# Pairwise products of a row: two pieces ahead of the loop, and a loop that begins with the third

## The chip, the core and the metric

The kernel runs on one core of a Trainium2 chip. The metric is the device time of one execution in microseconds; the profile that is read here was taken of one of the executions whose times are given. TensorE has no part in this kernel. The engines that matter are VectorE (DVE in the profile), ScalarE (ACT), SyncE (SP, which issues all the DMAs) and the sixteen DMA engines of the core.

## What is computed

The input is a matrix of 4096 rows and 256 columns in float32. For each row the outer product of the row with itself is formed, and its upper triangle is written out, row of the triangle after row of the triangle: 256 products with the first element, 255 with the second, and so on, 32,896 numbers in all.

```python
dot = jnp.einsum('bi,bj->bij', inputs, inputs)
iu, ju = jnp.triu_indices(d)
return dot[:, iu, ju]
```

4 MB are read and 539 MB are written. A run of the triangle (row i) is the tail of the input row, from element i on, times the one number x[i].

## The kernel before

**Tiling.** The 4096 rows are spread over 128 partitions, 32 to each. Two of them (REPEAT) are worked on at a time in every partition, so there are 16 groups. The width of 32,896 is cut into three pieces (PIECES, L115): c = 0 has 10,944 columns, c = 1 and c = 2 have 10,976 each. Each piece of a group is computed into one of two buffers, `places[0]` and `places[1]` (L128), and stored by one DMA of 11 MB. The first piece holds few long runs, the third many short ones.

**Sharing.** Of every piece, ACT computes the first runs and DVE the rest. `split` (L69) takes runs from DVE until DVE's time by a formula (L65: 68 ns and 1.046 ns an element, for one instruction over both rows) is within a budget of nanoseconds, or until ACT's time by its own formula (L74: 184 ns and 0.837 ns an element, one instruction for each of the two rows) is more than what is left to DVE. The budget is 0.9 times twice the columns (L204). A budget of 0 means an even split. DVE issues `tensor_tensor` products (L158), ACT an `activation` Copy with a scale (L170). Both read their own copy of the rows, `xv` and `xa`, which they refresh ahead of each c = 0 (L193 and L195).

**Order.** `rounds` (L178) writes out six pieces, two groups, for all engines. Piece p goes to buffer p mod 2. Before it is computed, DVE takes the buffer's semaphore `free` (L198), which the landing store of the piece two before has raised, and tells ACT by `go` (L199, L200). When DVE and ACT have marked their parts done (`v_done` L207, `a_done` L211), SP takes both marks and issues the store (L214). So at most two stores are under way, and a piece is computed while the store of the piece before it runs.

`rounds` is written out once ahead of the loop (L223) and is the body of a loop of seven passes over DVE, ACT and SP together (L224), whose head is put at the start of a code block on DVE and ACT (`head_slot`, L229). Ahead of the loop two things differ. The first two pieces wait for no buffer. And piece 0 is cut at columns 512, 1536 and 3584 (FIRST, L20), so that its first store can leave early; its four parts are shared evenly (L204, `start`), and each has its store. Piece 1 is shared by the budget of 0.9 like the rest. The input comes in three loads on SP (L138), the first of them only the rows of the first group; the others are waited for ahead of the second group (L188).

At the end SP takes both buffers' semaphores (L233), that is, waits for the last two stores, and lowers the loads' semaphores (L235).

Of the kernel before, what the change touches and what calls it, by code (L numbers as in the profile page):

```python
# [8 lines left out]
F32 = mybir.dt.float32  # L9
AF = mybir.ActivationFunctionType  # L10
ALU = mybir.AluOpType

P = 128
UNIT = 32
REPEAT = 2
PIECES = 3
PLACES = 2
ROUNDS = 2
BUDGET = 0.9
FIRST = [512, 1536, 3584]  # L20
ENGINES = OrderedEngineSet([mybir.EngineType.DVE, mybir.EngineType.Activation, mybir.EngineType.SP])


def even_borders(lo: int, hi: int, pieces: int) -> list[int]:
# [4 lines left out]
def runs(d: int, lo: int, hi: int) -> list:  # L29


    found, at = [], 0
    for i in range(d):
        a, b = max(at, lo), min(at + d - i, hi)
        if a < b:
            found.append((i, i + a - at, a, b - a))
        at += d - i
    return found


def vector_ops(block: list) -> list:

    ops, k = [], 0
    while k < len(block):
        i, j, at, n = block[k]
        m = 2 if k + 2 < len(block) and i == j else 1
        ops.append((block[k], m))  # L50
        k += m
    return ops


def interleave(block: list) -> list:


    half = len(block)
    while half and len(vector_ops(block[:half])) > len(vector_ops(block[half:])):
        half -= 1  # L60
    a, b = vector_ops(block[:half]), vector_ops(block[half:])
    return [op for k in range(max(len(a), len(b))) for ops in (a, b) for op in ops[k : k + 1]]


def vector_time(block: list) -> float:  # L65
    return sum(68 + 1.046 * REPEAT * n * m for (*_, n), m in vector_ops(block))


def split(block: list, budget: float) -> int:  # L69


    scalar, k = 0.0, 0
    while k < len(block):
        scalar += REPEAT * (184 + 0.837 * block[k][3])  # L74
        if vector_time(block[k:]) <= budget or scalar > vector_time(block[k + 1 :]):
            break
        k += 1
    return k


def window(ap: bass.AP, free: list) -> bass.AP:
    return bass.AP(ap.tensor, ap.offset, [list(ap.ap[0]), *free])


class Count:

    def __init__(self, ctx: ExitStack, nc, name: str):
        self.sem = ctx.enter_context(nc.semaphore(name))  # L90

    def take(self, engine, value: int):
        engine.wait_ge(self.sem, value).then_inc(self.sem, -value)  # L93


@with_exitstack
def kernel(
    ctx: ExitStack, tc: tile.TileContext, x: bass.AP, out: bass.AP
):

    nc = tc.nc
    n, d = x.shape  # L110
    width = out.shape[1]
    groups = n // (P * REPEAT)
    assert n % (P * REPEAT) == 0 and width == d * (d + 1) // 2 and width % UNIT == 0
    assert groups % ROUNDS == 0 and ROUNDS * PIECES % PLACES == 0
    borders = even_borders(0, width, PIECES)  # L115
    spans = list(zip(borders, borders[1:]))
    slot = max(b - a for a, b in spans)

    x_in = x.rearrange("(p g) d -> p (g d)", p=P)
    x_out = out.rearrange("(p h q r) c -> h q p r c", p=P, q=ROUNDS, r=REPEAT)  # L120

    each = REPEAT * d
    pool = ctx.enter_context(tc.tile_pool(name="all", bufs=1))
    xt = pool.tile([P, groups // ROUNDS, ROUNDS * each], F32, name="x")

    xv = pool.tile([P, each + 1], F32, name="xv")
    xa = pool.tile([P, each], F32, name="xa")
    places = [pool.tile([P, REPEAT, slot], F32, name=f"o{k}") for k in range(PLACES)]  # L128
    ctx.enter_context(tc.tile_critical())  # L129

    loads = [0, each, groups // 2 * each, groups * each]
    loaded = [ctx.enter_context(nc.semaphore(f"loaded{k}")) for k in range(len(loads) - 1)]
    free = [Count(ctx, nc, f"free{k}") for k in range(PLACES)]
    go, v_done, a_done = (Count(ctx, nc, name) for name in ("go", "v_done", "a_done"))
    v_own, a_own = (ctx.enter_context(nc.semaphore(name)) for name in ("v_own", "a_own"))

    for (a, b), sem in zip(zip(loads, loads[1:]), loaded):
        nc.sync.dma_start(xt.rearrange("p h d -> p (h d)")[:, a:b], x_in[:, a:b]).then_inc(sem, 16)  # L138

    class VectorWork:  # L140


        count = 0

        def add(self, ins, back: int = 1):
            if self.count > back:
                ins._wait_ge(v_own, self.count - back)
            ins.then_inc(v_own, 1)
            self.count += 1

        def end(self, back: int = 0):
            nc.vector.wait_ge(v_own, self.count)

    def vector_part(work: VectorWork, o, lo: int, block: list):
        for (i, j, at, length), m in interleave(block):
            at -= lo
            work.add(
                nc.vector.tensor_tensor(  # L158
                    o[:, :, at : at + m * length],
                    window(xv[:, j:], [[d, REPEAT], [1, m], [1, length]]),  # L160
                    window(xv[:, i:], [[d, REPEAT], [1, m], [0, length]]),
                    ALU.mult,
                )
            )

    def scalar_part(o, lo: int, block: list):
        ins = None
        for i, j, at, length in block:
            for r in range(REPEAT):
                ins = nc.scalar.activation(  # L170
                    o[:, r, at - lo : at - lo + length],
                    xa[:, r * d + j : r * d + j + length],
                    AF.Copy,
                    scale=xa[:, r * d + i : r * d + i + 1],
                )
        ins.then_inc(a_own, 1)

    def rounds(h, first: bool):  # L178

        work = VectorWork()  # L180
        for p in range(ROUNDS * PIECES):
            r, c = divmod(p, PIECES)
            k = p % PLACES
            lo, hi = spans[c]
            start = first and p == 0
            if c == 0:
                if first:
                    for sem in loaded[:1] if r == 0 else loaded[1:]:  # L188
                        nc.vector.wait_ge(sem, 16)
                        nc.scalar.wait_ge(sem, 16)  # L190
                x_now = xt[:, bass.ds(h, 1), r * each : (r + 1) * each]
                x_now = x_now.rearrange("p o d -> p (o d)")
                work.add(nc.vector.tensor_copy(xv[:, :each], x_now))  # L193
                work.end()
                nc.scalar.activation(xa, x_now, AF.Copy).then_inc(a_own, 1)  # L195
                nc.scalar.wait_ge(a_own, 1).then_inc(a_own, -1)
            if not (first and p < PLACES):
                free[k].take(nc.vector, 16 * stores[k])  # L198
                nc.vector.sem_inc(go.sem, 1)  # L199
                go.take(nc.scalar, 1)  # L200
            cuts = [lo, *(FIRST if start else []), hi]
            for a, b in zip(cuts, cuts[1:]):
                block = runs(d, a, b)
                share = split(block, 0.0 if start else BUDGET * REPEAT * (b - a))  # L204
                vector_part(work, places[k], lo, block[share:])
                work.end()
                nc.vector.sem_inc(v_done.sem, 1)  # L207
                if share:
                    scalar_part(places[k], lo, block[:share])
                    nc.scalar.wait_ge(a_own, 1).then_inc(a_own, -1)  # L210
                nc.scalar.sem_inc(a_done.sem, 1)  # L211
                v_done.take(nc.sync, 1)
                a_done.take(nc.sync, 1)
                nc.sync.dma_start(  # L214
                    x_out[bass.ds(h, 1), r, :, :, a:b].rearrange("o p r c -> p (o r) c"),
                    places[k][:, :, a - lo : b - lo],
                ).then_inc(free[k].sem, 16)
            stores[k] = len(cuts) - 1
        nc.vector.sem_inc(v_own, -work.count)

    stores = [0] * PLACES
    nc.vector.memset(xv[:, each:], 0.0)  # L222
    rounds(0, first=True)  # L223
    with nc.Fori(  # L224
        1,
        groups // ROUNDS,
        1,
        engines=ENGINES,
        head_slot={mybir.EngineType.DVE: 0, mybir.EngineType.Activation: 0},  # L229
    ) as h:  # L230
        rounds(h, first=False)
    for k in range(PLACES):
        free[k].take(nc.sync, 16)  # L233
    for sem in loaded:
        nc.sync.sem_inc(sem, -16)  # L235


# [25 lines left out]
```

## Time and profile before

| what | value |
|---|---|
| median of 4 executions | 1275.72 us (1275.56 to 1275.79) |
| the profiled execution | 1275.68 us, its span 1273.7 us |
| DVE, ACT busy | 952.5 us (1748 instructions), 535.2 us (1601) |
| stores of a whole piece, issue to landing, median | 31.9 us |
| DMA rate over the span | 426 GB/s |

The page begins with the busy time and its share of the span for every engine. Then the span is shown in forty slices; in the DMA row a digit is the mean busy share of the sixteen DMA engines in tenths, 9 for 90% or more. The part on queues gives the packets, their bytes and the time that they took; "instruction" packets bring program code of 8 KB each. A timeline row is a group of like instructions that follow each other: its start, its length, engine, line, what is written from what, how many, and in brackets the idle time of the engine before the first of them, with what ended it ("issue" is a wait for nothing that the profile shows). SPq, DVEq and ACTq are the sequencers of the engines, which wait and count semaphores. Besides, the trace holds a record for each DMA packet (start, length, bytes) and for each of the sixteen landing marks of a store.

### The profile page before, as it was taken

How to read it: one execution, taken by the hardware profiler on the slowest of the kernel's cores; microseconds unless marked ns; L12 is line 12 of the kernel's file. 1: busy time of each engine (PE TensorE's matmuls, PEld its weight loads, DVE VectorE, ACT ScalarE, POOL GpSimd, SP SyncE). 2: the span in 40 equal slices, each digit the busy share in tenths (PEclk: the TensorE clock that was granted, in tenths of full speed). 3: DMA queues.
4: the chain of work that ended last, by engine and by line, in shares of the span. 5: the costliest groups of instructions: out<-in, count | busy, mean ns of one | idle time of the engine just before them, and what ended most of it. 6: DMA issues, size and time to landing. Idle time of an engine off the chain costs nothing. (4 is left out here: it accounts for less than half of the span.)

```text
span 1273.7 us, 4059 instructions
## 1 busy us (share of the span) xinstructions
DVE 952.5 (75%) x1748; ACT 535.2 (42%) x1601; POOL 0.2 (0%) x4
## 2 busy tenths in 40 slices
DVE  8967787688867887678867787687877878678770
ACT  7524525245253442544326342263523625245250
POOL 0000000000000000000000000000000000000000
DMA  9999999999999999999999999999999999999997
GB/s 380 411 420 439 423 435 440 421 439 425 435 440 423 436 423 437 440 420 441 421 439 440 420 439 422 437 423 436 423 438 421 440 418 441 419 440 419 440 419 335
DMA packets 14314, 543.25 MB, mean 427 GB/s; under 512 B 864, under 2 KB 864, under 8 KB 1504
## 3 DMA queue, kind: packets, MB, share of 16 engines
q1 hardware_dynamic: 14304, 543.17, 99.2%
q14 instruction: 10, 0.08, 0.0%
HBM read 4.19 MB, written 538.97 MB: 426 GB/s over the span
## 5 line engine op out<-in xcount | busy, mean ns | idle before, releaser
L158 DVE TENSOR_TENSOR o<-xv 128x672 f32<-128x672 f32 (+27 forms) x1731 | 945.6, 631 | 268.9 <-DVEq L93 268.3
L170 ACT ACTIVATE o<-xa 128x253 f32<-128x253 f32 (+49 forms) x1584 | 523.8, 423 | 686.4 <-ACTq L93 685.6
L193 DVE COPY xv<-x 128x512 f32 (+1 forms) x16 | 6.8, 427 | 17.4 <-issue 8.2
L195 ACT ACTIVATE xa<-x 128x512 f32 (+1 forms) x16 | 10.1, 630 | 13.5 <-issue 6.1
L195 ACT ACT_TABLE_LOAD x1 | 1.3, 1283 | 0.9 <-SPq L129 0.9
L222 DVE MEMSET xv<- 128x1 f32 x1 | 0.1, 59 | 1.0 <-SPq L129 1.0
L250 POOL MEMSET const-bfloat16-1.0<- 128x1 bf16 x1 | 0.1, 101 | 0.0
L250 POOL MEMSET const-uint8-127<- 128x1 uint8 x1 | 0.1, 101 | 0.0
L250 POOL MEMSET const-float32-0.0<- 128x1 f32 x1 | 0.1, 98 | 0.2 <-issue 0.2
L250 POOL MEMSET const-float32-1.0<- 128x1 f32 x1 | 0.1, 98 | 0.0
## 6 DMA issues: line engine op xcount, KB each, us to landing
out_dram<-o SPq DMA_DIRECT2D x32, 10976.0 KB, 31.9
out_dram<-o SPq DMA_DIRECT2D x15, 10944.0 KB, 31.9
out_dram<-o SPq DMA_DIRECT2D x1, 7360.0 KB, 19.2
x<-in_r_inputs_dram SPq DMA_DIRECT2D x1, 2048.0 KB, 12.3
out_dram<-o SPq DMA_DIRECT2D x1, 2048.0 KB, 11.7
x<-in_r_inputs_dram SPq DMA_DIRECT2D x1, 1792.0 KB, 6.9
out_dram<-o SPq DMA_DIRECT2D x1, 1024.0 KB, 10.0
out_dram<-o SPq DMA_DIRECT2D x1, 512.0 KB, 9.7
```

Source lines behind the costliest of these rows:

```text
L158: nc.vector.tensor_tensor(o[:, :, at : at + m * length], window(xv[:, j:], [[d, REPEAT], [1, m], [1, length]]), window(xv[:, i:], [[d, REP ...
L170: ins = nc.scalar.activation(o[:, r, at - lo : at - lo + length], xa[:, r * d + j : r * d + j + length], AF.Copy, scale=xa[:, r * d + i : ...
L193: work.add(nc.vector.tensor_copy(xv[:, :each], x_now))
L195: nc.scalar.activation(xa, x_now, AF.Copy).then_inc(a_own, 1)
L222: nc.vector.memset(xv[:, each:], 0.0)
L250: nc = _bacc.Bacc("TRN2", target_bir_lowering=False, num_devices=1)
```

## The change

Ahead of the loop only pieces 0 and 1 are written out, and both are shared evenly between DVE and ACT; piece 0 keeps its four parts. The loop now has eight passes. A pass opens with pieces 2 to 5 of its two groups and goes on with pieces 0 and 1 of the next two groups; these last two stand in an If that the last pass jumps over. Each of the three engines has its own loop, so the program of each is written by a function of its own (`vector`, `scalar`, `sync`), and the waits on the second and third input loads come ahead of the loop. In the loop the budget is 0.95, 0.8 and 0.85 for the three kinds of piece instead of 0.9 for all. The stores of piece 0's four parts raise a semaphore `head`, and GpSimd, which had no part in the kernel, waits for it and raises `free[0]` in their place, so that the loop can always wait for one store.

In the built program, the first branch of ACT stands between its wait for the first load and the load of its activation table; formerly the table load came ahead of that wait. The loop has 243 instructions on DVE (242 before) and 249 on ACT (223 before); a piece takes, on DVE and ACT:

| piece | before: products on DVE, instructions on ACT | after, ahead of the loop | after, in the loop |
|---|---|---|---|
| c = 0 | 20, 18 (ahead of the loop 20, 34) | 20, 34 | 21, 14 |
| c = 1 | 26, 26 | 21, 44 | 23, 36 |
| c = 2 | 61, 54 | none | 59, 62 |

(These are counts of the sharing's own lists; the program has one product more in places.)

```diff
-ROUNDS = 2
-BUDGET = 0.9
+PASS = 6
+AHEAD = 2
+BUDGETS = [0.95, 0.8, 0.85]
...
+    def blocks(p: int, ahead: bool):
+        lo, hi = spans[p % PIECES]
+        cuts = [lo, *(FIRST if ahead and p == 0 else []), hi]
+        for a, b in zip(cuts, cuts[1:]):
+            block = runs(d, a, b)
+            k = split(block, 0.0 if ahead else BUDGETS[p % PIECES] * REPEAT * (b - a))
+            yield a - lo, b - lo, block[:k], block[k:], lo
+
+    def vector(h, pieces: range, ahead: bool):
+        for p in pieces:
+            if p % PIECES == 0:
+                v.add(nc.vector.tensor_copy(xv[:, :each], x_of(h, p // PIECES)), 0)
+                v.end()
+            if not ahead:
+                take(nc.vector, free[p % PLACES], 16)
+                nc.vector.sem_inc(go, 1)
+            for _, _, _, block, lo in blocks(p, ahead):
...
+                v.end().then_inc(v_done, 1)
+        v.restart()
+
+    def scalar(h, pieces: range, ahead: bool):
+        for p in pieces:
+            if p % PIECES == 0:
+                a.add(nc.scalar.activation(xa, x_of(h, p // PIECES), AF.Copy), 0)
+                a.end()
+            if not ahead:
+                take(nc.scalar, go, 1)
+            for _, _, block, _, lo in blocks(p, ahead):
...
+                a.end().then_inc(a_done, 1)
+        a.restart()
+
+    def sync(h, pieces: range, ahead: bool):
+        for p in pieces:
+            place = places[p % PLACES]
+            parts = list(blocks(p, ahead))
+            for lo, hi, *_, base in parts:
+                take(nc.sync, v_done, 1)
+                take(nc.sync, a_done, 1)
+                to = x_out[bass.ds(h, 1), p // PIECES, :, :, base + lo : base + hi]
+                nc.sync.dma_start(to.rearrange("o p r c -> p (o r) c"), place[:, :, lo:hi]).then_inc(
+                    free[p % PLACES] if len(parts) == 1 else head, 16
                 )
...
+    def all_pieces(engine, pieces_of):
+        pieces_of(0, range(AHEAD), True)
+        if engine is not nc.sync:
+            for sem in loaded[1:]:
+                engine.wait_ge(sem, 16)
+        kind = engine.engine
+        with nc.Fori(
+            0,
+            passes,
+            engines=OrderedEngineSet([kind]),
+            head_slot={kind: 0} if engine is not nc.sync else {},
+        ) as h:
+            pieces_of(h, range(AHEAD, PASS), False)
+            with engine.If(h < passes - 1):
+                pieces_of(nc.s_assert_within(h + 1, 0, passes - 1), range(AHEAD), False)
+
...
     nc.vector.memset(xv[:, each:], 0.0)
-    rounds(0, first=True)
...
+    for engine in (nc.vector, nc.scalar):
+        engine.wait_ge(loaded[0], 16)
+
+    take(nc.gpsimd, head, 16 * (len(FIRST) + 1))
+    nc.gpsimd.sem_inc(free[0], 16)
+    for engine, pieces_of in ((nc.vector, vector), (nc.scalar, scalar), (nc.sync, sync)):
+        all_pieces(engine, pieces_of)
     for k in range(PLACES):
-        free[k].take(nc.sync, 16)
+        take(nc.sync, free[k], 16)
     for sem in loaded:
-        nc.sync.sem_inc(sem, -16)
+        take(nc.sync, sem, 16)
```

## The prediction

> **What bounds the kernel now.** I read the page from the top: shares first, then the forty slices, then the DMA part.
>
> ```profile
> span 1273.7 us, 4059 instructions
> DVE 952.5 (75%) x1748; ACT 535.2 (42%) x1601; POOL 0.2 (0%) x4
> ...
> DMA  9999999999999999999999999999999999999997
> ...
> q1 hardware_dynamic: 14304, 543.17, 99.2%
> q14 instruction: 10, 0.08, 0.0%
> HBM read 4.19 MB, written 538.97 MB: 426 GB/s over the span
> ```
>
> No compute engine is full; the 16 DMA engines are, at 99.2% for 539 MB of results. So an edit is worth what it does to the stores, and the question is where the stores stop. The busy-time windows of the first 70 us answer it (columns: stretch, DVE, ACT, POOL busy, clock, DMA share, GB/s):
>
> ```profile
> 0.00:40.00 40.00, 35.65 (x49) 24.17 (x62) 0.20 (x4) 1.00 0.95 385
> 40.00:42.10 2.10, 1.75 (x5) 0.68 (x3) 0.00 (x0) 1.00 0.00 0
> 42.10:70.00 27.90, 19.82 (x63) 16.13 (x54) 0.00 (x0) 1.00 1.05 452
> ```
>
> From 40.0 to 42.1 us DMA carries nothing. The timeline says why, and shows the first loop entry further on (start, us, engine, line, then in brackets the idle time before):
>
> ```profile
> 4.25 36.79 DVE L158 TENSOR_TENSOR o<-xv 128x512 f32<-128x512 f32 x49
> ...
> 18.45 9.02 ACT L170 ACTIVATE o<-xa 128x7 f32<-128x7 f32 x26 [0.20 <-ACTq L210]
> 41.39 20.02 DVE L158 TENSOR_TENSOR o<-xv 128x484 f32<-128x484 f32 x62 [0.35 <-DVEq L93]
> ...
> 143.81 0.63 ACT L195 ACTIVATE xa<-x 128x512 f32 x1 [6.08 <-issue]
> 149.82 0.43 DVE L193 COPY xv<-x 128x512 f32 x1 [8.21 <-issue]
> ```
>
> DVE works on pieces 0 and 1 until 41.04; SP issues piece 1's store at 41.25 and its first packet runs at 42.14 (0.89 us from issue to packet). Piece 0's last packets had ended between 39.80 and 40.16. ACT was through with its part of piece 1 at 27.47 and idled 13.96 us: the piece was shared unevenly.
>
> After that the stores never stop. A late stretch:
>
> ```profile
> 1167.77 19.58 DVE L158 TENSOR_TENSOR o<-xv 128x988 f32<-128x988 f32 x20 [5.68 <-DVEq L93]
> ...
> 1193.92 19.70 DVE L158 TENSOR_TENSOR o<-xv 128x788 f32<-128x788 f32 x26 [6.58 <-DVEq L93]
> ...
> 1219.85 20.02 DVE L158 TENSOR_TENSOR o<-xv 128x484 f32<-128x484 f32 x62 [6.23 <-DVEq L93]
> ```
>
> Each piece starts when the store two before it has landed, 26.15 and 25.93 us apart, and DVE idles some 6 us in each. A store is issued about 20.4 us after the one two before it landed, so some 5.7 us before the one just ahead lands. The sixteen landing marks of each store show more: in the last third, fifteen DMA engines land 4.4 to 4.7 us before the sixteenth. That **laggard** is never without work from 42.1 us to its last packet at 1271.46: 47 stores in 1229.3 us, 26.155 us each, while the others need 26.01 when nothing holds them. The end of the kernel is the laggard's start plus its work. Compute that comes up to about 4.8 us later (5.7 less 0.89) costs it nothing.
>
> **The change, part by part**, against the profiled execution: span 1273.7, 1275.68 us with what lies around it (2.0 us), within 0.04 of the 1275.72 median.
>
> *Piece 1 shared evenly.* The kernel's own cost formula (L65 to L78), which met the trace within 0.2% for DVE on this piece (19.66 against 19.69 us) and 1.5% for ACT (8.88 against 9.02), now gives DVE 21 products for 26, 15.7 us for 19.7, and ACT 44 instructions for 26, 15.1 us. DVE started piece 1 at 21.34, so it ends at 37.05 and SP issues at 37.25 instead of 41.25. ACT started at 18.45 and ends near 34. Piece 0's last packets run until 39.9, so the hole closes; what DVE wins beyond it is wait. The laggard's idle time went from 39.9 or 40.16 (its packets cannot be told apart yet) to 42.15: 2.0 to 2.25, taken as **-2.2 us**.
>
> *ACT's start.* In the built program ACT waits for the first load and takes one branch before its table load (1.28 us, formerly over by 2.19, under the load that ends the wait at 3.79). Copy and first mark come 1.4 us later, near 5.9, and the 512-column store leaves about 0.3 us after 5.84. The input loads keep DMA busy until 13 us: **0**. The cover ends if ACT is over 3 us late on the last part of piece 0 (it ended at 18.24, DVE at 21.24).
>
> *Loop entry before piece 2.* It costs 6.08 us on ACT and 8.21 on DVE in the rows above, the code's two first blocks on their way (six of the ten instruction packets fall into 120 to 160 us). Now it comes at 37.1 for DVE. Bounds: 0.2 us, the gap before an ordinary copy, to 8.2. I take 8.2, the only entry seen, so piece 2 starts at 45.4 instead of 41.39. Its DVE share is 18.57 us by the formula, 18.9 at the trace's ratio; its store is issued near 64.5 and runs at 65.4. Piece 1's store, started at 39.9, lasts until 65.9: hidden with 0.5 us to spare, **0**, and 1 us per us beyond. POOL's new hop (it turns `head` into free[0]) adds two semaphore steps of some 0.1 us, ahead of a start that already waits for code: 0.
>
> The Trainium skill, "Runtime: NRT & Kernel Launch", section "Instruction fetch mechanics", speaks against the change: a taken branch whose target lies outside a window of two 16 KiB pages of 256 instructions stalls for a fetch, so a loop cut by an If may pay at each turn. By that page's figure the new loops, 243 instructions on DVE and 249 on ACT, fit into one page, and the sum stays as it is.
>
> *The If and the turn of the loop.* A turn costs 0.8 us on DVE now (0.77 idle ahead of the copy, 0.24 without a turn), inside its 6 us. No instruction packet comes after 234 us: the 242 and 223 instructions of the old loops stay put; 243 and 249 should. One more compare-and-branch and register step each pass are below 0.3 us, within the same idle time: 0.
>
> *New shares 0.95, 0.8, 0.85.* By the formula DVE gets 20.7, 17.4 and 18.6 us (was 19.5, 19.7, 19.7), ACT 5.5, 12.4 and 18.2. Piece 0's store is issued 1.1 us later, the others 1 to 2 us earlier; the laggard's 4.8 us cover all of it: 0 on the waits. But the number of instructions has a price. The laggard's packets last 1618 to 1632 ns, and 1641 to 1669 for about ten packets while the instruction-rich third piece (62 DVE, 54 ACT) is computed. Its stores come at 26.39 us then and 26.12 otherwise; 71 more records of all engines in the richest piece than in the leanest make 3.8 ns each, a fit of single packets 2.7. The new program runs some 270 more, about 220 of them ACT's. Bounds 0 (if only DVE's, which stay level, count) to 1.0; I take 2.2 ns each, between the fit and nothing, **+0.6**.
>
> *End.* SP takes five marks as before, POOL joins the closing wait: one 0.06 us step, +0.1 with its drain.
>
> Sum: -2.2 + 0.6 + 0.1 = -1.5; 1275.7 - 1.5 = **1274.2 us**.
>
> **The rivals.**
>
> *Instructions cost the laggard nothing*, or only DVE's do (36 products fewer, -0.1): -2.2 + 0.1 - 0.1, 1273.5 us, and 0.3 less if the hole is 2.25 and the slower first packets after it (1650 ns for 1627, two rounds) go too: 1273.2. For: a fit is no proof. Against: the pattern repeats with every third piece.
>
> *The hole is filled and given back*: the laggard's pace makes up for a later start, 1275.7. For: nothing but the pace's unknown cause. Against: it held 26.155 us over 47 stores.
>
> *Code for piece 2 comes later*: two fetches in a row, 5.5 us apart like the instruction packets at 142.0 and 147.4. Piece 2 starts at 50.9, its store's first packet is at 70.9 against 65.9: 5 us of new hole, 1279.2. It decides once the entry takes over 8.7 us. For: DVE and ACT enter 3 us apart, in queues full of stores. Against: fewer instructions precede the loop, and the packets in flight are 1.1 us long, not 1.63.
>
> *Slower: the loops are fetched anew each pass.* The first loop pass of before prices it: eight instruction packets at 120 to 234 us, and landings 27.78, 26.52 and 26.70 apart instead of 25.9, 3.3 us on another DMA engine. Eight passes give that engine 47 x 25.9 + 8 x 3.3 = 1243.7 us of work, 14.4 over the laggard's: near 1288. It decides above 1.5 us of fetching per pass. For: ACT's loop grew by 26 to 249. Against: DVE's 242 stayed.
>
> **How the numbers follow.** Forecast 1274.2: 0.66; no price per instruction 1273.5: 0.16; given back 1275.7: 0.06; later code 1279.2: 0.06; fetched anew 1288: 0.06. The range leaves out the last two: 1273.0 to 1276.0. About 0.2% (2.55 us) is what a measurement can tell from no change, so faster needs less than 1273.2 and slower more than 1278.3. The forecast's own gain is below that. Faster 0.07 (under half of the second case), slower 0.10 (most of the last two), same 0.83.
>
> **What would show it.** The windows at 38 to 44 us full of DMA; piece 1's store issued near 37.2; DVE's idle time at its loop entry under 8.7 us and piece 2's store issued by 65; no instruction packets after the first pass; landings still 26.1 to 26.2 us apart, with one engine 4 us behind at the end. Wrong would be: a hole near 66 us, landings further apart in every pass, or a laggard that isn't the same at the end.

## The result

The changed kernel takes **1273.61 us** (median of 40 executions, 1273.47 to 1273.80); the kernel before took 1275.70 beside it (60 executions, 1275.52 to 1275.82). The ratio is 0.9984 with a 95% interval of 0.9979 to 0.9988: 2.09 us less, surely below 1, but short of the 0.2% (2.55 us) that was set as the line for "faster". The forecast of 1274.2 was 0.6 us too slow.

The profile after, the page first (share and count of each engine, the forty slices, the queues):

```profile
span 1271.6 us, 4308 instructions
...
DVE 915.3 (72%) x1712; ACT 606.4 (48%) x1837; POOL 0.2 (0%) x4
...
DMA  9999999999999999999999999999999999999998
...
q1 hardware_dynamic: 14304, 543.17, 99.3%
q14 instruction: 7, 0.05, 0.0%
HBM read 4.19 MB, written 538.97 MB: 427 GB/s over the span
```

The span is 2.1 us shorter, like the time. The stores' queue went from 99.2% to 99.3%, there are seven instruction packets for ten, and work has gone from DVE to ACT: 36 DVE instructions fewer, 236 of ACT more.

The windows of the first 70 us (stretch, DVE, ACT, POOL busy, clock, DMA share, GB/s; a packet counts where it starts, so a short stretch can show more than 1):

```profile
0.00:40.00 40.00, 32.78 (x47) 30.40 (x80) 0.20 (x4) 1.00 0.96 390
40.00:42.10 2.10, 0.00 (x0) 0.00 (x0) 0.00 (x0) 1.00 1.29 551
42.10:70.00 27.90, 20.86 (x63) 20.51 (x67) 0.00 (x0) 1.00 1.00 428
```

The stretch from 40.0 to 42.1 us, in which DMA carried nothing, now carries 551 GB/s. It is the engines that do nothing in it. The timeline of the first pass (start, us, engine, line; L185 holds the products that were L158, L206 ACT's that were L170):

```profile
4.04 1.28 ACT L199 ACT_TABLE_LOAD   x1 [4.04 <-DMA x<-in_r_inputs_dram]
...
4.36 32.89 DVE L185 TENSOR_TENSOR o<-xv 128x512 f32<-128x512 f32 x45
...
6.11 28.86 ACT L206 ACTIVATE o<-xa 128x253 f32<-128x253 f32 x78
...
44.07 18.88 DVE L185 TENSOR_TENSOR o<-xv 128x468 f32<-128x468 f32 x60 [6.82 <-DVEq L135]
44.10 18.39 ACT L206 ACTIVATE o<-xa 128x98 f32<-128x98 f32 x62 [9.12 <-ACTq L135]
...
68.45 20.75 DVE L185 TENSOR_TENSOR o<-xv 128x996 f32<-128x996 f32 x22 [4.83 <-DVEq L135]
...
139.66 0.43 DVE L175 COPY xv<-x 128x512 f32 x1 [0.62 <-DVEq L155]
```

DVE ends piece 1 at 37.25 (4.36 + 32.89), 3.79 us earlier than before, and SP issues its store at 37.46. Then DVE waits 6.82 us: 6.1 of them, from 37.66 to 43.77, are the branch into the loop. Piece 2 starts at 44.07, its store is issued at 63.35, and piece 1's packets end from 66.0 on. With the 0.89 us from issue to packet, 1.76 us were to spare. The copy at 139.66, behind the branch of the If, shows 0.62 us of idle time. The turn of the loop comes later in the pass: its branch runs from 190.66 to 191.00, and DVE then waits for a store until 198.43. The late stretch of the same run:

```profile
1166.09 20.75 DVE L185 TENSOR_TENSOR o<-xv 128x996 f32<-128x996 f32 x22 [6.82 <-DVEq L135]
...
1192.15 17.52 DVE L185 TENSOR_TENSOR o<-xv 128x768 f32<-128x768 f32 x24 [5.31 <-DVEq L135]
...
1218.16 18.88 DVE L185 TENSOR_TENSOR o<-xv 128x468 f32<-128x468 f32 x60 [8.50 <-DVEq L135]
```

The starts are 26.06 and 26.01 us apart, and DVE still idles 5 to 8.5 us ahead of each piece: the stores pace the loop as before.

Where did the 2.09 us come from? Three numbers per run tell: the *pace* (mean of the last 30 distances between landings of stores), the *anchor* (last landing less 47 paces: where the even row of stores begins), and the *tail* (last landing to the end of the span).

| run | instructions | span | anchor | pace | tail |
|---|---|---|---|---|---|
| before | 4059 | 1273.68 | 42.72 | 26.154 | 1.74 |
| after | 4308 | 1271.61 | 40.62 | 26.163 | 1.33 |
| difference in us | | -2.07 | -2.10 | +0.42 (47 x 0.009) | -0.41 |

So read, the hole gave 2.10, the instructions took 0.42, and the end gave 0.41; the anchor takes the pace of the last 30 stores for all 47. The landings agree. The last mark of a store comes 1.9 to 2.0 us earlier than before around 500 us and 1.7 earlier at the end. The median of the sixteen marks is 2.2 us earlier from piece 1 up to 640 us, and 0.5 to 1.2 at the end, where only the last mark sets the time.

### The profile page after: what moved, and what is told of

Read it like the earlier page. It is cut to its first block, busy times and chain, and to the rows that moved or that the text cites. A ratio compares the mean times of both kernels' runs of the same rounds, so it can differ in the third digit from the quotient of the medians.

```text
span 1271.6 us, 4308 instructions
## 1 busy us (share of the span) xinstructions
DVE 915.3 (72%) x1712; ACT 606.4 (48%) x1837; POOL 0.2 (0%) x4
## 3 DMA queue, kind: packets, MB, share of 16 engines
q1 hardware_dynamic: 14304, 543.17, 99.3%
## 5 line engine op out<-in xcount | busy, mean ns | idle before, releaser
L185 DVE TENSOR_TENSOR o<-xv 128x736 f32<-128x736 f32 (+61 forms) x1695 | 908.4, 620 | 311.7 <-DVEq L135 311.0
L206 ACT ACTIVATE o<-xa 128x198 f32<-128x198 f32 (+44 forms) x1820 | 595.0, 419 | 621.1 <-ACTq L135 620.6
```

What stands on the lines that cost most here:

```text
L185: nc.vector.tensor_tensor(places[p % PLACES][:, :, at : at + m * length], window(xv[:, j:], [[d, REPEAT], [1, m], [1, length]]), window(xv ...
L206: ins = nc.scalar.activation(places[p % PLACES][:, r, at - lo : at - lo + length], xa[:, r * d + j : r * d + j + length], AF.Copy, scale=x ...
```

## Experiments

Each has its own run of the kernel before on the same chip; differences are against that one (1275.45 to 1275.72). "Anchor", "pace" and "tail" are those of the table above. They are put in order of the questions. The intervals of the ratios reach about 0.1% (some 1.2 us) to either side, though executions of one kernel lie within 0.4 us of each other. So a difference of half a microsecond between two experiments rests on the pace, anchor and tail of their traces, and is weaker evidence than a step of 2 us.

### Is it the hole alone? One line in the kernel before

```diff
-                share = split(block, 0.0 if start else BUDGET * REPEAT * (b - a))
+                share = split(block, 0.0 if first and p < PLACES else BUDGET * REPEAT * (b - a))
```

> The kernel before with one edit: piece 1, ahead of the loop, is shared evenly between DVE and ACT. Theory (the hole of DMA at 40.0 to 42.1 us is what the change removed, and the lagging DMA engine sets the end): piece 1's store is issued near 37.4 instead of 41.25, the hole is gone, the last landing comes 2.1 us earlier, 1273.6 us (1273.3 to 1273.9); the loop's code entry is where it was. Rival (the gain comes from the new loop, its shares or its shorter end, and a filled hole is given back by the laggard): 1275.5 to 1275.8.

Measured: 1273.26 us, -2.23; ratio 0.9983 (0.9974 to 0.9992). Its windows:

```profile
38.00:40.00 2.00, 0.00 (x0) 0.00 (x0) 0.00 (x0) 1.00 1.25 536
40.00:42.10 2.10, 1.22 (x3) 1.18 (x5) 0.00 (x0) 1.00 0.92 397
```

DMA runs on at 40 us. The anchor is 40.33 (-2.39), pace and tail are those of before, and the last mark of each store stays 2.4 us earlier from 460 us to the end. So one even share of piece 1 is worth as much as the whole rewrite: the other parts of the change, taken together, give nothing that shows.

### The rewrite without the even share of piece 1

```diff
-            k = split(block, 0.0 if ahead else BUDGETS[p % PIECES] * REPEAT * (b - a))
+            k = split(block, 0.0 if ahead and p == 0 else (0.9 if ahead else BUDGETS[p % PIECES]) * REPEAT * (b - a))
```

> The changed kernel with one edit: piece 1, ahead of the loop, gets the old budget of 0.9 (DVE 26 products, ACT 26 instructions). Theory: the hole is back, DMA idle from 40.0 to 42.1 us, and the entry into the loop now starts at 41.6 on DVE, so that piece 2 starts near 48 and its store is issued near 67.3, 0.9 us more to its first packet at 68.2, about when piece 1's store ends (42.1 + 26.0 = 68.1); last landing 2.1 us later than in the changed kernel, 1275.7 us in all (1275.4 to 1276.2). Rival (loop and shares make the gain): 1273.6.

Measured: 1275.62, +0.13; ratio 1.0001 (0.9992 to 1.0010). The window in which DMA stood still (columns as above):

```profile
39.80:41.80 2.00, 1.05 (x3) 0.00 (x0) 0.00 (x0) 1.00 0.00 0
```

and two rows of its timeline, DVE's end of piece 1 and start of piece 2:

```profile
29.38 11.48 DVE L185 TENSOR_TENSOR o<-xv 128x748 f32<-128x748 f32 x16
...
46.04 18.89 DVE L185 TENSOR_TENSOR o<-xv 128x468 f32<-128x468 f32 x60 [5.19 <-DVEq L135]
```

DVE works on piece 1 until 40.86 again, no packet starts between 39.8 and 41.8, and the gain is gone. The anchor is 42.56, as before; pace 26.163 and tail 1.33 are those of after. The new loop by itself trades 0.4 us of instructions against 0.4 us at the end.

### Does the number of instructions cost DMA time? 1216 fewer

```diff
                 block = runs(d, a, b)
+                if c == 2:
+                    block = [(0, 1, lo, 32)] + [(i, j, lo + 32 + at, n_) for i, j, at, n_ in runs(d, *spans[0])]
```

> The kernel before, but the third piece of each group is computed with the run list of the first one (and one short run more), so its numbers are wrong; the busy time of DVE stays about 19.6 us a piece, ACT's falls to 7.6, and every third piece has 20 products and 20 ACT instructions instead of 61 and 54, some 1200 instructions less in all. Theory (the laggard's packets take longer with each instruction that runs, 2.2 to 3.8 ns): its stores all come 26.0 to 26.1 us apart and the pattern of 26.35 every third store is gone, last landing 2.7 to 4.6 us earlier, 1271.1 to 1273.0 us. Rival (the laggard is slow by itself, or slow where the store's addresses lie): the pattern stays, 1275.7 us.

Measured: 1271.64, -3.85; ratio 0.9970 (0.9959 to 0.9981). From the page:

```profile
span 1269.8 us, 2843 instructions
...
DVE 945.4 (74%) x1076; ACT 399.7 (31%) x1057; POOL 0.2 (0%) x4
```

This kernel leaves out the third piece's own products, but the bytes stored are the same and the hole at 40 us is still there. Yet it is 3.85 us faster: 3.2 ns for each record that is gone. The pace fell to 26.077 (47 x 0.077 = 3.6), and the slow store of every third piece (26.4 in before) went with the short runs. This is an effect on the DMA side: DVE was no less busy to speak of (945 us for 952).

### Instructions that touch no data: 3600 semaphore steps on GpSimd

```diff
+    idle = ctx.enter_context(nc.semaphore("idle"))
+    with nc.Fori(0, 30, 1, engines=OrderedEngineSet([mybir.EngineType.Pool])):
+        for _ in range(60):
+            nc.gpsimd.sem_inc(idle, 1)
+            nc.gpsimd.sem_inc(idle, -1)
     stores = [0] * PLACES
```

> The kernel before, and beside it GpSimd runs a loop of 30 turns with 120 semaphore steps each on a semaphore of its own, 3600 records that touch no data and that nobody waits for, over in about the first quarter of the span. Theory (each record of any engine costs the laggard): 3600 at 3.1 ns, 11 us more, 1286.7 us; on another DMA engine that is now the quicker one by 7 us in the whole, 4 us more, 1279.5. Rival (only instructions that compute, or that DVE and ACT issue, count): 1275.5 us.

Measured: 1286.53, +11.04; ratio 1.0086 (1.0071 to 1.0102). From the page:

```profile
span 1284.5 us, 7723 instructions
...
DVE 952.3 (74%) x1748; ACT 535.1 (42%) x1601; POOL 0.2 (0%) x4
...
q1 hardware_dynamic: 14304, 543.17, 98.4%
q14 instruction: 12, 0.10, 0.0%
```

An idle engine counting its own semaphore makes the kernel 11 us longer: 3.0 ns for each of 3664 records more. Landings come 27.2 to 27.6 us apart while that loop runs (its last record is at 294.3 us), and 26.15 in the mean at the end; the anchor is 10.8 us later and the pace that of before. Reading of memory by DVE and ACT is ruled out as the cause, since these instructions read none, and so is the fetching of code: twelve instruction packets for ten. What remains is something that happens for each instruction, whether DVE, ACT or GpSimd runs it. One DMA engine of the sixteen is slowed: while the loop runs, the sixteenth landing mark falls up to 6.9 us behind the fifteenth. That it is the writing of the profile's own records would fit, but that is a guess; no run here tells it apart. Whether the price is paid where nothing is recorded stays open.

With the run before this one and the pairs below, the laggard's price comes to about 3.4 ns for a DVE product, 2.4 ns for an ACT instruction and 3.0 ns for a semaphore step. This is an estimate, fitted to the runs; with it each run's change of pace comes out within 0.1 us over 47 stores.

### The old budget of 0.9 in the new loop

```diff
-BUDGETS = [0.95, 0.8, 0.85]
+BUDGETS = [0.9, 0.9, 0.9]
```

> The changed kernel with the old budget of 0.9 for all three pieces in the loop: some 64 products more on DVE and 224 instructions fewer on ACT, 160 records fewer in all. Theory (3.1 ns for each record of any engine, as 1216 fewer gave 3.85 us): 0.5 us less than the changed kernel, 1273.1 us (1272.9 to 1273.3). Rival A (only DVE's instructions count): 0.2 us more, 1273.8. Rival B (the unequal budgets themselves are a gain, by issuing the stores of the second and third piece earlier): 1274.0 and more.

Measured: 1272.84, -2.65; ratio 0.9979 (0.9970 to 0.9988). Against after's own -2.09 that is 0.56 better, with 186 instructions fewer (218 on ACT, while DVE has 32 more); the pace is back at 26.154, which is 0.4 us, and the anchor is 0.25 earlier, for a reason that stays open. The two intervals overlap, but by the traces the change's new shares cost some half a microsecond and bring nothing.

### Fewer instructions still: two budgets

```diff
-BUDGETS = [0.95, 0.8, 0.85]
+BUDGETS = [1.08, 1.08, 0.9]
```

> The changed kernel with budgets of 1.08, 1.08 and 0.9: DVE 23, 30 and 61 products, ACT 4, 10 and 54 instructions, 33 fewer per three pieces, 500 in all; piece 2 behind the loop entry keeps 20 us, so that its store comes in time (issue near 64.0 us, where the run with 22.9 us of it left DMA idle from 65.5 to 68). Theory: 500 at 3.1 ns, 1.6 us less than the changed kernel, 1272.0 us (1271.7 to 1272.5), no idle DMA near 66. Rival (stores that are issued 23.5 us after the landing come too late for the laggard): landings over 26.2 us apart, 1273.6 us or more.

Measured: 1272.96, -2.53; ratio 0.9980 (0.9971 to 0.9989). The pace fell, to 26.141 (47 x 0.022 = 1.0 us less than after, where 1.6 was expected), but the anchor is 0.5 us later. Piece 3, the first c = 0 of the loop, is the longest on DVE:

```profile
68.15 23.52 DVE L185 TENSOR_TENSOR o<-xv 128x1016 f32<-128x1016 f32 x24 [3.70 <-DVEq L135]
```

Its store was issued at 92.04, too late: the first DMA engines had landed piece 2's store at 91.99. A piece that long is still hidden in the late passes, where fifteen engines land 0.5 to 1.0 us before the sixteenth. In the first pass the laggard is not behind yet.

```diff
-BUDGETS = [0.95, 0.8, 0.85]
+BUDGETS = [1.0, 1.0, 0.9]
```

> The changed kernel with budgets of 1.0, 1.0 and 0.9: DVE 22, 28 and 61 products, ACT 10, 16 and 54 instructions; against the flat 0.9, four products more on DVE and 18 instructions fewer on ACT per three pieces. Theory (the runs so far give about 3.4 ns for a product on DVE and 2.4 for an instruction on ACT; pieces of 22 us are still early enough in the first passes, those of 23.5 were not and cost 0.5 us there): 16 times 29.6 ns, 0.5 us less than the flat 0.9, 1272.4 us. Rival (any piece longer than 20 us costs in the first passes): 1272.8 or more.

Measured: 1272.88, -2.84; ratio 0.9977 (0.9968 to 0.9986). From the page:

```profile
span 1270.8 us, 3927 instructions
...
DVE 1016.2 (80%) x1819; ACT 441.3 (35%) x1349; POOL 0.2 (0%) x4
```

Pace 26.147, anchor 40.56. Of the kernels that do the whole work it has the largest difference, with 381 instructions fewer than after. Its interval lies below 1, but overlaps that of after. It is only 0.2 us ahead of the flat 0.9, where 0.5 was expected; these two intervals overlap as well. Its pace is worth 0.3 us against the flat 0.9, and its anchor is 0.2 later, so the rival, a small cost of pieces over 20 us in the first passes, isn't ruled out.

### A longer loop: 273 instructions on DVE

```diff
-BUDGETS = [0.95, 0.8, 0.85]
+BUDGETS = [1.05, 1.05, 1.05]
```

This makes DVE's loop 273 instructions long.

> The changed kernel with budgets of 1.05 for all three pieces: DVE 23, 29 and 66 products, ACT 6, 12 and 34 instructions, 22.9 us of DVE a piece by the formula. Two things move. Some 45 instructions less per three pieces, 700 in all, which by 2.2 to 3.8 ns each give 1.5 to 2.7 us. And DVE's loop grows from 243 to 273 instructions. Theory A (a loop of up to 512 instructions stays where it is, and compute that comes 3 us later is covered by the laggard's 4.8 us): no instruction packets after the first pass, 1270.9 to 1272.1 us. Theory B (over 256 instructions the code is fetched anew each pass): two to four instruction packets in every pass, DVE idle 5 us and more at each turn of the loop, its stores late by more than the cover; 1276 to 1300 us.

Measured: 1273.91, -1.58; ratio 0.9987 (0.9978 to 0.9996). Neither theory's price came. Instruction packets run at 22.4, 39.1, 41.6, 48.8, 107.4 and 179.3 us, and the next at 1235.0, at the loop's end: nothing is fetched anew. The Trainium skill, "Runtime: NRT & Kernel Launch", section "Instruction fetch mechanics", speaks of a window of two pages of 256 instructions each; 273 instructions that stay agree with that. The pace is 26.134, 1.4 us less than after over 47 stores. What spoils it is in the windows at 64 us:

```profile
64.00:65.50 1.50, 1.50 (x7) 0.00 (x0) 0.00 (x0) 1.00 1.08 468
65.50:68.00 2.50, 1.69 (x8) 0.00 (x0) 0.00 (x0) 1.00 0.04 18
68.00:69.00 1.00, 0.86 (x1) 0.80 (x2) 0.00 (x0) 1.00 1.65 702
```

Piece 2 now takes DVE some 23 us, its store is issued at 67.16, and DMA has nothing to start for 2.5 us: the anchor is 42.34, 1.7 later than after's. This is the new hole that the rival of the later code told of, reached by longer work in place of later code.

### How much later may piece 2 start? Eleven copies, then twenty-five

```diff
                 engine.wait_ge(sem, 16)
+        if engine is nc.vector:
+            for _ in range(11):
+                v.add(nc.vector.tensor_copy(xv[:, :each], x_of(0, 0)), 0)
+            v.end()
+            v.restart()
         kind = engine.engine
```

> The changed kernel, but DVE copies the first rows into xv eleven times more ahead of its loop (the same numbers), which takes about 6 us; so it enters the loop, and starts piece 2, 6 us later, near 50 us. Theory (early on no DMA engine lags yet, so that cover ends where piece 1's store ends, 66.0 us): piece 2's store, issued near 69.4, has its first packet near 70.3, DMA is idle from 66.1 to 70.3 and the whole is 4.0 to 4.7 us longer than the changed kernel, 1277.4 to 1278.1 us. Rival (the 4.8 us of cover of the late stores hold from the start): 1.5 us or less, 1273.4 to 1274.9.

Measured: 1273.64, -2.08; ratio 0.9984 (0.9974 to 0.9993), the same as after. From the timeline:

```profile
37.48 5.04 DVE L237 COPY xv<-x 128x512 f32<-128x512 f32 x11 [0.32 <-DVEq L155]
44.00 18.89 DVE L185 TENSOR_TENSOR o<-xv 128x468 f32<-128x468 f32 x60 [1.48 <-DVEq L135]
```

This did not test what it was meant to: five microseconds of copies moved piece 2 by -0.07. The branch came at 42.74 in place of 37.66, and the loop went on at 43.69 in place of 43.77. So the entry is not a price that each branch pays. It is a wait until the code has arrived, at about 43.7 us, whatever DVE does meanwhile. Instruction packets started at 40.3 and 41.9 us here, and at 40.5 and 42.0 in after. In the rewrite with the uneven piece 1 the second one started at 43.96, and DVE went on at 45.74: in all three DVE goes on 1.8 us after that packet's start. What sets the packet's own time isn't shown. With 25 copies for 11 the code is there first:

> As the late entry before it, with 25 copies of xv instead of 11. With 11 copies DVE was done at 42.5 us and the loop's code was there at 43.7 us, as without them, so nothing was late. 25 copies end near 49.0, and piece 2 starts near 50.2 (or later, if the branch then waits for code). Theory (in the first passes the cover of piece 2's store ends where piece 1's store ends, 66.0 us less the 0.9 from issue to packet): issue near 69.5, first packet 70.4, DMA idle from 66.1 on but for one or two engines, 4.0 to 4.6 us longer than the changed kernel, 1277.6 to 1278.2 us. Rival (the 4.8 us of cover of the late stores hold from the start): 1.5 us longer or less, up to 1275.1.

Measured: 1277.26, +1.81 against before, +3.90 against after's -2.09; ratio 1.0014 (1.0005 to 1.0023). Two rows of its timeline, the copies and piece 2:

```profile
37.29 11.50 DVE L237 COPY xv<-x 128x512 f32<-128x512 f32 x25 [0.32 <-DVEq L155]
49.88 18.88 DVE L185 TENSOR_TENSOR o<-xv 128x468 f32<-128x468 f32 x60 [1.09 <-DVEq L135]
```

and a window of the same run:

```profile
66.00:70.00 4.00, 3.52 (x16) 3.23 (x11) 0.00 (x0) 1.00 0.00 0
```

Piece 2 starts at 49.88, 5.81 later than in after. Less the 1.76 us that after had to spare, 4.05 us should show, and 3.9 do; the window shows them as four microseconds in which no packet starts. So the early cover ends where piece 1's store ends, and beyond it each microsecond costs one.

### What shortened the end? GpSimd in the closing wait

Both experiments begin with the even share of the first one, and add only steps.

```diff
+    step = ctx.enter_context(nc.semaphore("step"))
+    nc.gpsimd.sem_inc(step, 1)
+    nc.gpsimd.wait_ge(step, 1).then_inc(step, -1)
     stores = [0] * PLACES
```

> The kernel before with the even piece 1, and GpSimd takes two steps on a semaphore of its own at the start, so that it joins the program's closing wait as in the changed kernel. Theory (the closing part is 0.44 us shorter when GpSimd is in it: 1.33 us from the last landing to the end for 1.76): 1272.8 us, 0.44 less than with the even piece 1 alone. Rival (the closing part is shorter for another reason, such as the place of SP's last instructions in its program): 1273.3.

Measured: 1273.27, -2.22; ratio 0.9983 (0.9974 to 0.9992). The tail is 1.75 as in before, so GpSimd's part in the closing wait is not what shortens it: that theory fell. The records of SP behind the last landing show a stop of 0.44 us, ahead of the ninth instruction from SP's last wait on. With GpSimd's one more wait it falls on another instruction, at the same count. In after there is no such stop. A place in SP's program would explain that:

```diff
+    step = ctx.enter_context(nc.semaphore("step"))
+    for _ in range(6):
+        nc.sync.sem_inc(step, 1)
+        nc.sync.wait_ge(step, 1).then_inc(step, -1)
     stores = [0] * PLACES
```

> The kernel before with the even piece 1, and SP has twelve semaphore steps more in its program, right behind the input loads, where it has nothing to do. Theory (the closing part of the old programs holds a stop of 0.44 us ahead of the ninth SP instruction from the last take on, whatever that instruction is, so it hangs on the place in SP's program): the stop moves twelve places ahead, into the wait for the last store, and the whole is 0.4 us shorter than with the even piece 1 alone, 2.65 us below the kernel before, 1273.1 us where that takes 1275.7 (1272.8 where it takes 1275.5). Rival (the stop belongs to the closing instructions themselves): 2.2 us below.

Measured: 1273.32, -2.13; ratio 0.9983 (0.9974 to 0.9992). The stop is gone, the tail is 1.22, and SP's steps up to the ninth follow each other every 0.06 to 0.08 us. So the stop hangs on the place in SP's program. But the time is no shorter, since the last landing came 0.55 us later than without the steps. An instruction packet of 8 KB that had come behind the end, at 1271.1 us, now ran at 301.4; the laggard fell back 0.3 to 0.55 us from about 410 us on. Whether the one made the other isn't settled. That a shorter tail is a gain shows better in two other runs: the new loop with the flat 0.9 has nearly the pace and the anchor of the one-line run (26.154 and 40.37, for 26.154 and 40.33), a tail of 1.33 for 1.74, and is 0.42 us ahead of it, each against its own kernel before. SP's program differs in length in the changed kernel too (eleven stores written out for fifteen), so the stop may be out of the way there for the same reason; no run tests that in the changed kernel.

## Why the prediction was right or wrong

**What bounds the kernel** was read rightly: the stores set the time, and one hole of 2 us was there to be had. The one-line run shows it from one side, the uneven rewrite from the other. Besides the hole, the laggard's pace counts, and 1216 instructions fewer were worth more (3.85 us) than the hole. The lead of the fifteen engines was put at 4.4 to 4.7 us in the last third; the landing marks show that it grows, from 3.5 to 4.65 us there, and that it is at most 1.5 us up to 500 us.

**The hole, -2.2.** Measured -2.10 at the anchor. DVE's end (37.05 forecast, 37.25 measured) and the issue (37.25, 37.46) were met within 0.2 us.

**ACT's start, 0.** The table load ran from 4.04 to 5.32 behind the wait; the first store left at 6.13 (5.84 before, 0.3 later as worked out), and ACT ended its share at 34.97. Nothing of it reached the stores.

**Loop entry, 0.** The cost was right, its reason only partly. The 8.2 us of the old entry were taken over as if each branch cost so much; DVE waited 6.1 us, ACT 0.4, and the late-entry run shows a wait for a packet. Piece 2 started at 44.07 for 45.4, and 1.76 us were to spare for 0.5. The stated price of 1 us per us beyond the cover was right (3.9 for 4.05).

**The If and the turn, 0.** Right: 0.62 us ahead of the copy behind the If and 0.34 from the turn's branch to the next instruction, both within idle time; no packet in later passes.

**New shares: waits 0, instructions +0.6.** The waits were right, for the shares chosen. The sentence that the laggard's 4.8 us cover any piece holds late in the run alone: at 1.08 piece 3, at 1.05 piece 2 ran out of cover in the first pass. The price was right in kind, +0.42 for 0.6: 249 more records at 1.7 ns for 270 at 2.2. The two runs that carry it are the one with 1216 instructions fewer (-3.85) and the GpSimd loop (3664 more, +11.04).

**End, +0.1: the term that failed.** "POOL joins the closing wait: one 0.06 us step, +0.1 with its drain". Measured -0.41: a 0.44 us stop among SP's closing instructions, which the prediction had not looked at, is gone. GpSimd has no part in it: with GpSimd in the closing wait of the old program the stop stayed. Twelve more steps in SP's program took it away there, which makes the place in SP's program the likely cause in the changed kernel too; that itself was not tested. The miss of 0.6 us adds up: 0.5 from the end, 0.2 from the instructions, less 0.1 from the hole.

**The rivals.** *No price per instruction* named 1273.5, within 0.1 us of what came, and is still wrong: the price was paid, and the end gave it back. A total that fits is no proof of its terms. *The hole given back*: no, in the one-line run the last marks stay 2.4 us earlier to the end; in the changed kernel 1.7 are left, and the difference to 2.1 is the price of its instructions. *Later code for piece 2*: the code came earlier; the price of that rival was seen when the start was delayed by hand (piece 2 at 49.88, +3.9) and when piece 2 was lengthened (+1.7). *Loops fetched anew*: no, not even at 273 instructions.

## What to carry to other kernels

Where a DMA queue is over 99% busy, look for the stretches in which it is not; the largest gain of a rewrite may lie in one of them, and one line may close it. Cover that is there late in a run, when one DMA engine lags, need not be there in the first pass, so size the pieces by the early stores. With stores as the bound, fewer and longer instructions win a little (2 to 3 ns each here), on DVE, ACT and GpSimd alike.

## What was not expected of the hardware

- Instructions of DVE, ACT and GpSimd slow one of the sixteen DMA engines: 3664 records more, nearly all of them semaphore steps on an idle GpSimd, took 11.0 us; 1216 instructions fewer on DVE and ACT gave 3.9.
- The wait at a loop's entry ends when the code's packet has come: 6.1 us on DVE and 0.4 on ACT in the same program, 0.95 when DVE branches 5 us later.
- A stop of 0.44 us stands at a fixed count among SP's closing instructions, and is gone when SP has twelve more steps ahead of them (tail 1.22 us for 1.74).
- A loop of 273 instructions on DVE isn't fetched anew over its passes.
